# Layer 1's attention in two passes of scores instead of one pass and transposed probabilities

## The chip, the cores and the metric

The program runs on one core of one Trainium2 chip. The metric is device microseconds of one execution, and a kernel's time is the median of several runs. Every operand is fp32.

## The reference, cut to what matters

The input x has 8 batches of 512 tokens of width 128. Two blocks follow each other. Each has an adaptive layer norm, an attention, a second norm and a feed-forward network. The change concerns the attention of the second block (layer 1): 16 heads of width 8, causal, and with a bias that decays with distance.

```python
std_logits = einsum('bhqd,bhkd->bhqk', q, k) * scale
incidence = einsum('bqhp,bkhp->bhqk', read_lines, J_write)      # 6 numbers per head and token
weights = decays[:, None, None] ** diffs_pos[None] * past       # past: key before query
bias = incidence * weights[None] * bias_scale[None, :, None, None]
...
softmax over the causal keys of (std_logits + bias), then times v, then w_out
```

## The kernel before, in words

The stages run one after the other: setup, layer 0's attention, layer 0's quantized feed-forward network, layer 1's attention, layer 1's feed-forward network. X, with all tokens, stays in the on-chip memory from start to end. A scheduler orders the stages except layer 1's attention, whose order is written out by hand in `attention1` (inside `manual_schedule`): on each engine the instructions run in the order in which the Python code issues them.

Layer 1's attention works on 8 batches by 4 groups of four heads. `front1`, once a batch and cut into pieces at its `yield`s, makes the norm, the projections, and from them three packs: for q and k, 32 columns a head, of which 6 hold the lines, 8 the head's numbers (`KR` = 14 in use) and the rest zeros; for v, 9 columns a head, the ninth of them ones, so that the sum of the probabilities falls out of the same matmul.

For a group, `prep1` (L546) turns the packs of q and k, 128x128 at a time, so that the four heads lie at partitions 0, 32, 64 and 96; ACT copies the results to `q1T` and `k1T` (L558, L560); POOL multiplies decays into `qd` (L563) and into four `kd`, one for each tile of 128 queries (L572). `lines1` multiplies the lines of each diagonal tile on PE (`pi`, L584); DVE multiplies by the diagonal's weights (`bias`, L590), and POOL writes -1e30 above the diagonal (L594). `scores1` (L605) computes scores with queries in rows. A head contracts 14 rows only, and heads at different partitions can run side by side in the array.

The 512 queries of a head are four tiles; causality gives tile t the first t+1 blocks of 128 keys. They are grouped in three units: tiles 0 and 1 together, tile 2, tile 3. `quad` takes two PSUM tiles of two banks for four heads. `softmax1` adds the bias of the diagonal tile on DVE (L622, L626), reduces to the negated maximum on DVE (L629), and takes the exponential on ACT, one instruction for each head and tile, with the maximum as the activation's bias (L633). For the product with v the keys must lie in rows: `turn1` transposes the probabilities on PE (`pr1T`, L646), ACT copies them back (`p1T`, L652), and `values1` (L663) contracts them with the pack of v. There, four heads write four strips of 32 partitions of `po`. `outcome1` copies `po` to `og`, turns it (`ogT`, L159), divides by the sums, and after the fourth group multiplies by w_out (L695) and adds to X.

PSUM has eight banks: four for the two pairs of `quad`, two for `tp`, two for `acc`. In the hand-written order, the scores of one unit stand on PE ahead of the transposes of the unit before it, two units being in flight; the parts of `front1` for the next batch and of `outcome1` for the group before lie in between.

Of the kernel before, what the change touches and what calls it, by code (L numbers as in the profile page):

```python
# [32 lines left out]
def kernel(ctx: ExitStack, tc: tile.TileContext, a: dict, out: bass.AP):  # L33
# [3 lines left out]


    ps = ctx.enter_context(tc.tile_pool(name="ps", bufs=2, space=PSUM))
    four = None  # L40
# [4 lines left out]
    def quad(name):  # L45

        return [
            four.tile([P, 2, 512], F32, tag=f"pair{i}", bufs=1, name=f"{name}_{i}")
            for i in range(2)
        ]  # L50

    def tp(name):
        return ps.tile([P, 512], F32, tag="tp", bufs=2, name=name)

    def acc(name):
        return ps.tile([P, 512], F32, tag="acc", bufs=2, name=name)
# [20 lines left out]
    banks = tc.tile_pool(name="ps_l0", bufs=4, space=PSUM)  # L77
# [64 lines left out]
    def ln_norm(pool, tag, stats, b):  # L142
        mv, rstd = stats[b // (B // 2)]
        n = pool.tile(
            [P, NT, D], F32, tag="n", bufs=1 if tag == "a1" else 2, name=f"n_{tag}_{b}"
        )
        for t in range(NT):
            i = (b % (B // 2)) * NT + t
            nc.vector.tensor_scalar(
                n[:, t, :], X[:, b * NT + t, :], mv[:, i, 0:1], rstd[:, i : i + 1],  # L150
                ALU.subtract, ALU.mult,
            )
        return n
# [241 lines left out]
    def lines_setup(pool):  # L395
# [12 lines left out]
        io = pool.tile([P, 384], F32, tag="pT", bufs=8, name="io")  # L408
# [4 lines left out]
        iq = pool.tile([P, P], F32, tag="pT", bufs=8, name="iq")  # L413
# [4 lines left out]
        df = pool.tile([P, P], F32, tag="pT", bufs=8, name="df")  # L418
# [24 lines left out]

        packs = {}
        for i in range(2):
            for name in ("q", "k"):
                pk = pool.tile(
                    [P, NT, H, 32], F32, tag=f"pack_{name}{i}", bufs=1, name=f"pack_{name}{i}"
                )
                nc.gpsimd.memset(pk, 0.0)  # L450
                packs[name, i] = pk
# [6 lines left out]
    UNITS = (((0, 0), (1, P)), ((2, 0),), ((3, 0),))  # L458

    def front1(pool, st, b, stats, bqs, packs):  # L460
# [6 lines left out]
        st["wo", b] = wo = pool.tile([P, D], F32, tag="wo", name=f"wo1_{b}")  # L467
# [14 lines left out]
        for t in range(NT):  # L482
            cur = hT[:, 1 + t * P : 1 + (t + 1) * P]
            pb = acc(f"pb_{b}_{t}")
            nc.tensor.matmul(
                pb[:, 0:64], lhsT=hT[:, t * P : (t + 1) * P], rhs=wC, start=True, stop=True
            )
            nc.tensor.matmul(pb[:, 64:256], lhsT=cur, rhs=wB, start=True, stop=True)
            nc.scalar.copy(pw[:, :, t, :], pb[:, 0:256].rearrange("p (i r) -> p i r", i=2))
            if t % 2:  # L490
                yield
# [13 lines left out]
        nc.gpsimd.tensor_sub(ln, ln, m2)  # L505
        for t in range(NT):
            cur = hT[:, 1 + t * P : 1 + (t + 1) * P]
            pa = acc(f"pa_{b}_{t}")
# [11 lines left out]
            if t == 1:  # L520
                nc.scalar.activation(m2, ln, AF.Square)
                ss = pool.tile([P, nln], F32, tag="ss", bufs=1, name=f"ss_{b}")
                nc.vector.tensor_reduce(ss, m2, AX.X, ALU.add)
                nc.vector.tensor_scalar_max(ss, ss, 1e-24)
            yield

        lg = pool.tile([P, nln], F32, tag="lg", bufs=1, name=f"lg_{b}")
        nc.scalar.activation(lg, ss, AF.Ln)
        rn = pool.tile([P, NT, 2, H], F32, tag="rn", bufs=1, name=f"rn_{b}")
        rv = rn.rearrange("p t w h -> p (t w h)")  # L530
        nc.scalar.activation(rv, lg, AF.Exp, scale=-0.5)
        nc.gpsimd.tensor_mul(lg, rv, rv)
        nc.gpsimd.tensor_mul(lg, lg, ss)
        nc.gpsimd.tensor_scalar(lg, lg, -0.5, 1.5, ALU.mult, ALU.add)
        nc.gpsimd.tensor_mul(rv, rv, lg)
        nc.gpsimd.tensor_mul(
            rn[:, :, 1, :], rn[:, :, 1, :], bsc.unsqueeze(1).to_broadcast([P, NT, H])
        )
        yield
        lnv = ln.rearrange("p (t w h) e -> p t w h e", t=NT, w=2)  # L540
        over = lambda w: rn[:, :, w, :].unsqueeze(3).to_broadcast([P, NT, H, NL])
        nc.gpsimd.tensor_mul(kp[:, :, :, 0:NL], lnv[:, :, 0], over(0))

        nc.gpsimd.tensor_mul(qp[:, :, :, 0:NL], lnv[:, :, 1, :, ::-1], over(1))
        yield

    def prep1(pool, st, b, g, packs, dk, dq):

        qp, kp = packs["q", b % 2], packs["k", b % 2]
        pq, pk = tp(f"pqT_{b}_{g}"), tp(f"pkT_{b}_{g}")  # L550
        for src, dst in ((qp, pq), (kp, pk)):
            for t in range(NT):
                nc.tensor.transpose(
                    dst[:, t * P : (t + 1) * P],
                    src[:, t, 4 * g : 4 * g + 4, :].rearrange("p h e -> p (h e)"), ident,
                )
        qT = pool.tile([P, T], F32, tag="qT", name=f"q1T_{b}_{g}")
        nc.scalar.copy(qT, pq)  # L558
        kT = pool.tile([P, T], F32, tag="kT", name=f"k1T_{b}_{g}")
        nc.scalar.activation(kT, pk, AF.Copy, scale=rowsgn[:, 0:1])  # L560

        qd = pool.tile([P, NT, P], F32, tag="qd", name=f"qd_{b}_{g}")
# [4 lines left out]
        kd = []  # L567
        for t in range(NT):
            kd.append(
                pool.tile([P, (t + 1) * P], F32, tag=f"kd{t}", name=f"kd{t}_{b}_{g}")  # L570
            )
            nc.gpsimd.tensor_mul(kd[t], kT[:, : (t + 1) * P], dk[:, g, 384 - t * P :])  # L572
        st["prep", b, g] = qT, kT, qd, kd

    def lines1(pool, st, b, g, wdiag):


        qT, kT = st["prep", b, g][:2]
        pi = quad(f"pi_{b}_{g}")
        for t in range(NT):  # L580
            tile_t = slice(t * P, (t + 1) * P)
            for j in range(4):
                rl = slice(32 * j, 32 * j + NL)
                nc.tensor.matmul(  # L584
                    pi[j // 2][:, j % 2, tile_t], lhsT=qT[rl, tile_t], rhs=kT[rl, tile_t],
                    start=True, stop=True,
                )
        st["bias", b, g] = bias = pool.tile([P, 4, NT, P], F32, tag="bias", name=f"bias_{b}_{g}")
        for j in range(4):
            nc.vector.tensor_mul(  # L590
                bias[:, j], pi[j // 2][:, j % 2].rearrange("p (t k) -> p t k", k=P),
                wdiag[:, 4 * g + j, :].unsqueeze(1).to_broadcast([P, NT, P]),
# [6 lines left out]
    def scores1(st, b, g, u):  # L599
        qT, kT, qd, kd = st["prep", b, g]  # L600
        st["s", b, g, u] = s = quad(f"s1_{b}_{g}_{u}")
        for t, at in UNITS[u]:
            for j in range(4):
                rk = slice(32 * j, 32 * j + KR)
                nc.tensor.matmul(  # L605
                    s[j // 2][:, j % 2, at : at + (t + 1) * P], lhsT=qd[rk, t, :],
                    rhs=kd[t][rk, :], start=True, stop=True,
                )

    def softmax1(pool, st, b, g, u, i):  # L610

        s, bias, unit, two = st["s", b, g, u][i], st["bias", b, g], UNITS[u], slice(2 * i, 2 * i + 2)
        if i == 0:
            st["pr", b, g, u] = (
                pool.tile([P, 4, T], F32, tag="pr", name=f"pr1_{b}_{g}_{u}"),
                pool.tile([P, 2, 4], F32, tag="nm", bufs=4, name=f"nm1_{b}_{g}_{u}"),
            )
        pr, nm = st["pr", b, g, u]
        if len(unit) == 2:

            diag = s.rearrange("p j (n c) -> p j n c", c=2 * P)[:, :, :, 0:P]
            nc.vector.tensor_add(diag, diag, bias[:, two, 0:2, :])  # L622
        else:
            t = unit[0][0]
            diag = s[:, :, t * P : (t + 1) * P]
            nc.vector.tensor_add(diag, diag, bias[:, two, t, :])  # L626
        for n, (t, at) in enumerate(unit):
            end = at + (t + 1) * P
            nc.vector.tensor_reduce(nm[:, n, two], s[:, :, at:end], AX.X, ALU.max, negate=True)  # L629
        for j in (2 * i, 2 * i + 1):  # L630
            for n, (t, at) in enumerate(unit):
                end = at + (t + 1) * P
                nc.scalar.activation(  # L633
                    pr[:, j, at:end], s[:, j % 2, at:end], AF.Exp, bias=nm[:, n, j : j + 1]
                )

    def width1(u):
        t, at = UNITS[u][-1]
        return at + (t + 1) * P

    def turn1(pool, st, b, g, u, j):

        pr, width = st["pr", b, g, u][0], width1(u)
        pt = tp(f"pr1T_{b}_{g}_{u}_{j}")
        for c in range(0, width, P):
            nc.tensor.transpose(pt[:, c : c + P], pr[:, j, c : c + P], ident)  # L646
        pT = pool.tile([P, T], F32, tag="pT", bufs=8, name=f"p1T_{b}_{g}_{u}_{j}")
        st["pT", b, g, u, j] = pT, pt

    def turned1(st, b, g, u, j):  # L650
        pT, pt = st["pT", b, g, u, j]
        nc.scalar.copy(pT[:, : width1(u)], pt[:, : width1(u)])  # L652
# [247 lines left out]
```

## Time and profile before

| what | value |
|---|---|
| median of 3 runs | 1687.89 us (1687.46 to 1688.57) |
| the profiled execution's own time | 1685.65 us |
| its span | 1683.6 us |
| granted TensorE clock over the span | 0.803 |
| span from 528.6 to 1360.0 us (layer 1's attention) | PE busy 710.27, DVE 427.78, ACT 482.70, POOL 293.20 us, clock 0.76 |
| first and last copy of `po` to `og` (32 of them) | start at 530.0 and 1359.3 us |
| matmul records of `pr1T`, of `s`, of `po` in layer 1's attention | 1280, 1024, 2560 |
| copies of `p1T` on ACT | 384 |

How to read it: the profile lists, for each engine, when an instruction started and how long it took, and what ended the idle time before it. PE is TensorE, PEld its loading of weights. Matmuls are pipelined, and their recorded lengths overlap, so busy time on PE is more than its work; the distance from one start to the next shows the rate. The clock of a stretch is the share of TensorE's full speed that was granted there. The first stages, up to about 460 us, and the last one, from about 1360 us, stand outside the attention of layer 1.

### The profile page before, as it was taken

To read this page: it belongs to the slowest core of one execution; us is meant where nothing else is said; L and a number is where in the kernel's file an instruction comes from. 1 tells how busy PE (TensorE), PEld (TensorE's weight loads), DVE (VectorE), ACT (ScalarE), POOL (GpSimd) and SP (SyncE) were. 2 spreads that over 40 slices of the span, in tenths; PEclk is the share of its full clock that TensorE was granted. 3 is DMA by queue.
4 is the path that set the end of the run, shared out by engine and by line. 5 is a ranking of instruction groups with operands and counts; after the bars stand their busy time and mean duration, and the time that the engine had idled before them with its cause. 6 is when DMAs were issued, how large, how long until landed. Compare 5 with 4: busy or idle time off the path is not lost.

```text
span 1683.6 us, 22090 instructions
## 1 busy us (share of the span) xinstructions
PE 1317.8 (78%) x8644; PEld 814.0 (48%) x8644; DVE 753.9 (45%) x1545; ACT 719.1 (43%) x1440; POOL 428.5 (25%) x524
## 2 busy tenths in 40 slices
PE   4699343553448888988888888888888889999999
PEld 4355132433335555555555555555555544444444
DVE  3866854454425555455555555455545541003000
ACT  3243211221346555655555665555556552114111
POOL 0210322111254424343343244342432200000000
PEclk9799677676757777677687877777777789999999
DMA  6000000000000000000000000000000000000000
GB/s 178 1 1 0 1 0 0 0 0 0 0 0 1 1 1 1 1 1 1 1 1 1 2 1 1 1 1 1 1 1 2 1 1 1 13 7 7 7 7 12
DMA packets 14317, 10.96 MB, mean 7 GB/s; under 512 B 1862, under 2 KB 12678, under 8 KB 14214
## 3 DMA queue, kind: packets, MB, share of 16 engines
q1 hardware_dynamic: 12054, 8.02, 1.6%
q10 hardware_dynamic: 2160, 1.54, 0.3%
q8 instruction: 68, 1.11, 0.3%
q14 instruction: 35, 0.29, 0.1%
HBM read 7.46 MB, written 2.10 MB: 6 GB/s over the span
## 4 chain that ended last, share of the span: by engine, by line
PE 52%; ACT 13%; DVE 4%; POOL 2%; issue 2%; ACTq 0%; POOLq 0%; DVEq 0%
PE ph L814 13%; PE pr1T L646 11%; PE s L605 9%; ACT pr L633 7%; PE po L663 4%; ACT p1T L652 2%; PE pi L584 2%; PE ogT L159 2%; PE pg L794 2%; PE py L825 2%; PE pu L795 2%; DVE nm L629 1%; PE pa L509 1%; ACT k1T L560 1%; PE py L695 1%
## 5 line engine op out<-in xcount | busy, mean ns | idle before, releaser
L652 ACT COPY p1T<-pr1T 128x384 f32<-128x384 f32 (+1 forms) x384 | 195.7, 522 | 247.7 <-PE pr1T L646 247.4
L646 PE MATMUL pr1T<-ident,pr 128*128 128x128 f32 x1280 | 273.0, 369 | 23.7 <-ACT p1T L652 16.9
L605 PE MATMUL s<-kd,qd 14*128 14x128 f32 (+3 forms) x1024 | 196.5, 600 | 80.2 <-ACT pr L633 62.1
L646 PEld LDWEIGHTS pr1T<-ident,pr 128*128 128x128 f32 x1280 | 198.8, 187 | 110.8 <-ACT p1T L652 49.9
L633 ACT ACTIVATE pr<-s,nm 128x128 f32<-128x128 f32 (+3 forms) x512 | 234.6, 547 | 3.0 <-DVE nm L629 2.9
L814 PE MATMUL ph<-g,c_h 128*128 128x512 f32 x512 | 222.0, 592 | 0.0
L629 DVE TENSOR_REDUCE nm<-s 128x2 f32<-128x256 f32 (+3 forms) x256 | 205.0, 821 | 6.6
L814 PEld LDWEIGHTS ph<-g,c_h 128*128 128x128 f32 x512 | 96.4, 190 | 116.7 <-issue 116.7
L605 PEld LDWEIGHTS s<-kd,qd 14*128 14x128 f32 x1024 | 69.7, 224 | 154.4 <-ACT pr L633 69.9
L594 POOL TENSOR_SCALAR_AFFINE_SELECT bias<-bias 128x512 f32<-128x512 f32 x128 | 77.1, 635 | 208.2 <-DVE bias L590 208.2
L818 ACT ACTIVATE g<-ph,c_scl 128x512 f32<-128x512 f32 x64 | 44.0, 688 | 196.3 <-PE ph L814 196.3
L590 DVE TENSOR_TENSOR bias<-pi,wdiag 128x512 f32<-128x512 f32 x128 | 79.4, 683 | 104.3 <-PE pi L584 104.3
L357 PE MATMUL yTp<-ident,q_xn_y 128*88 128x128 f32 x128 | 27.5, 388 | 117.3 <-DVE q_xn_y L252 117.3
L829 DVE TENSOR_TENSOR X<-X,py 128x512 f32<-128x512 f32 x8 | 5.5, 687 | 243.3 <-PE py L825 243.3
L663 PE MATMUL po<-p1T,pack_v 128*32 128x128 f32 x2560 | 108.8, 317 | 0.0
L572 POOL TENSOR_TENSOR kd<-k1T,dk 128x128 f32<-128x128 f32 (+3 forms) x128 | 106.4, 861 | 0.0
L663 PEld LDWEIGHTS po<-p1T,pack_v 128*32 128x32 f32 x2560 | 77.0, 126 | 29.2 <-issue 27.1
L622 DVE TENSOR_TENSOR s<-s,bias 128x512 f32<-128x512 f32 x64 | 44.4, 694 | 85.0 <-PE s L605 85.0
L357 PEld LDWEIGHTS yTp<-ident,q_xn_y 128*88 128x88 f32 x128 | 21.6, 178 | 123.3 <-issue 121.9
L626 DVE TENSOR_TENSOR s<-s,bias 128x256 f32<-128x256 f32 x128 | 54.4, 425 | 58.0 <-PE s L605 53.1
L563 POOL TENSOR_TENSOR qd<-q1T,dq 128x512 f32<-128x512 f32 x32 | 40.4, 1263 | 124.4 <-ACT q1T L558 124.4
L807 POOL TENSOR_TENSOR w3b<-c_w,gs 128x512 f32<-128x512 f32 x8 | 10.1, 1268 | 241.5 <-PE py L825 241.5
(232 smaller groups left out, 1847.8 us busy)
## 6 DMA issues: line engine op xcount, KB each, us to landing
X<-in_x SPq DMA_DIRECT2D x8, 256.0 KB, 6.1
c_h<-in_h SPq DMA_DIRECT2D x2, 1024.0 KB, 10.3
out_x<-X SPq DMA_DIRECT2D x8, 256.0 KB, 2.3
c_wmod<-in_wmod ACTq DMA_DIRECT2D x2, 384.0 KB, 7.0
c_w<-in_w SPq DMA_DIRECT2D x3, 256.0 KB, 3.0
c_wqkv<-in_wqkv ACTq DMA_DIRECT2D x1, 192.0 KB, 7.1
c_bA<-in_bA ACTq DMA_DIRECT2D x1, 192.0 KB, 5.2
c_wA<-in_wA SPq DMA_DIRECT2D x1, 192.0 KB, 4.6
```

Of the source, the lines that this page charges most:

```text
L357: nc.tensor.transpose(pt[:CH0, c * P : (c + 1) * P], q[:, t, c, :], ident)
L572: nc.gpsimd.tensor_mul(kd[t], kT[:, : (t + 1) * P], dk[:, g, 384 - t * P :])
L590: nc.vector.tensor_mul(bias[:, j], pi[j // 2][:, j % 2].rearrange("p (t k) -> p t k", k=P), wdiag[:, 4 * g + j, :].unsqueeze(1).to_broadca ...
L594: nc.gpsimd.affine_select(out=bias[:, j], in_=bias[:, j], compare_op=ALU.is_ge, fill=NEG, base=0, pattern=[[0, NT], [-1, P]], channel_mult ...
L605: nc.tensor.matmul(s[j // 2][:, j % 2, at : at + (t + 1) * P], lhsT=qd[rk, t, :], rhs=kd[t][rk, :], start=True, stop=True,)
L626: nc.vector.tensor_add(diag, diag, bias[:, two, t, :])
L629: nc.vector.tensor_reduce(nm[:, n, two], s[:, :, at:end], AX.X, ALU.max, negate=True)
L633: nc.scalar.activation(pr[:, j, at:end], s[:, j % 2, at:end], AF.Exp, bias=nm[:, n, j : j + 1])
L646: nc.tensor.transpose(pt[:, c : c + P], pr[:, j, c : c + P], ident)
L652: nc.scalar.copy(pT[:, : width1(u)], pt[:, : width1(u)])
L663: nc.tensor.matmul(po[32 * j : 32 * j + 32, t * P : (t + 1) * P], lhsT=vp[:, k, h * VW : h * VW + 32], rhs=st["pT", b, g, u, j][0][:, at + ...
L814: nc.tensor.matmul(ph, lhsT=w[:, k, c * P : (c + 1) * P], rhs=src[:, k, :], start=(k == 0), stop=(k == NC1 - 1),)
```

## The change

The probabilities are no longer transposed. Scores are computed twice. The first pass has queries in rows, as before, and serves for the maxima only: DVE adds the bias and reduces, and the negated maximum of each query and head is written into column 14 (`KR`) of the pack of q (`maxima1`). The pack of k has a column of ones there. The pack of q is then turned once more (`prep_m`), and multiplied by the decays as before (`qm`). The second pass (`scores2`) has keys in rows: 15 rows are contracted, so that the maximum is subtracted within the matmul. Before it, `bank2` writes the diagonal tiles' bias into the same PSUM bank, turned by a PE transpose, and `scores2` accumulates on it. One exponential then covers both heads of a pair and all of a unit (`exp1`), and its result goes straight to `values1`.

The units become tile 3, tiles 2 and 0 together, tile 1. PSUM: two double banks `px` for the first pass and the lines, one double bank `py` for the second pass, one bank `tp`, one bank `po`. `acc` goes: its users in `front1` and `outcome1` take `tp`. Every step is for a pair of heads instead of four.

The order: a round has eight steps; in it the second pass of one group, the first pass of the next and the preparation of the one after run together.

```diff
+    UNITS = (((3, 0),), ((2, 0), (0, 3 * P)), ((1, 0),))
...
+    def bank2(st, b, g, u, i):
+        st["p", b, g, u, i] = p = pair("py", 1, f"s2_{b}_{g}_{u}_{i}")
+        bias = st["bias", b, g, i]
+        for j in range(2):
+            for n, (t, at) in enumerate(UNITS[u]):
+                nc.tensor.matmul(
+                    p[:, j, at + t * P : at + (t + 1) * P], lhsT=bias[:, j, t, :], rhs=ident,
+                    is_transpose=True, start=(n == 0), stop=False, skip_group_check=True,
+                )
+
+    def scores2(st, b, g, u, i):
+        p = st["p", b, g, u, i]
+        for t, at in UNITS[u]:
+            for k in range(t + 1):
+                for j in range(2):
+                    rk = slice(32 * (2 * i + j), 32 * (2 * i + j) + KR + 1)
+                    nc.tensor.matmul(
+                        p[:, j, at + k * P : at + (k + 1) * P],
+                        lhsT=st["kd", b, g][t][rk, k * P : (k + 1) * P],
+                        rhs=st["qm", b, g][rk, t, :], start=False, stop=True,
+                        skip_group_check=True,
+                    )
+
+    def exp1(pool, st, b, g, u, i):
...
+        nc.scalar.activation(pr[:, :, :end], st["p", b, g, u, i][:, :, :end], AF.Exp)
...
+        for n in range(-2, len(groups) + 1):
+            past, second, first, new = (at(n + i) for i in range(-1, 3))
+            if n % NG == NG - 1 and n // NG + 2 < B:
+                front = front1(pool, st, n // NG + 2, stats, bqs, packs)
+            for s in range(8):
+                if s == 0 and second:
+                    prep_m(pool, st, *second, packs, dq)
+                elif s in (1, 5, 6, 7):
+                    next(front, None)
+                elif s == 3 and new:
+                    prep_q(pool, st, *new, packs, dq)
+                elif s == 4 and new:
+                    prep_k(pool, st, *new, packs, dk)
+                if s in (2, 5, 6, 7):
+                    next(ended, None)
+                i = s % 2
+                two = (*second, s // 2 - 1, 1 - i) if second and s > 1 else None
+                if two:
+                    bank2(st, *two)
+                if s < 6 and first:
+                    scores1(st, *first, s // 2, i)
+                elif s > 5 and new:
+                    lines1(st, *new, i)
+                if two:
+                    scores2(st, *two)
+                    exp1(pool, st, *two)
+                if s < 6 and first:
+                    maxima1(st, *first, s // 2, i, packs)
+                elif s > 5 and new:
+                    bias1(pool, st, *new, i, wdiag)
+                if s == 0 and past:
+                    values1(st, *past, 2, packs)
+                    ended = outcome1(pool, st, *past)
+                    next(ended)
+                elif s in (4, 6) and second:
+                    values1(st, *second, s // 2 - 2, packs)
```

Smaller edits go with it. The norm of layer 1's attention moves from DVE to ACT (`ln_norm`, four activations a batch). `front1` computes the lines' reciprocal norms ahead of the projection of q, k and v instead of behind it, so that Square, Ln and Exp stand together on ACT. `kd` has three buffers, `bias` five of a pair each. The activation table with both Ln and Exp is loaded ahead of the attention and held in program order. The PSUM pools `tp` and `acc`, which lasted for the whole program, are now made in each stage, with the same number of banks outside of layer 1's attention.

## Prediction

> **What bounds the kernel now.** I read the page first: engine shares, then the slices with the clock that TensorE was granted, then the groups.
>
> ```profile
> PE 1317.8 (78%) x8644; PEld 814.0 (48%) x8644; DVE 753.9 (45%) x1545; ACT 719.1 (43%) x1440; POOL 428.5 (25%) x524
> ...
> PEclk9799677676757777677687877777777789999999
> ...
> PE 52%; ACT 13%; DVE 4%; POOL 2%; issue 2%; ACTq 0%; POOLq 0%; DVEq 0%
> ...
> L652 ACT COPY p1T<-pr1T 128x384 f32<-128x384 f32 (+1 forms) x384 | 195.7, 522 | 247.7 <-PE pr1T L646 247.4
> L646 PE MATMUL pr1T<-ident,pr 128*128 128x128 f32 x1280 | 273.0, 369 | 23.7 <-ACT p1T L652 16.9
> ```
>
> PE is busiest and leads the chain that ended last; the copies of p1T wait for PE, not the reverse. From slice 12 to 32, layer 1's attention, the clock is about 0.76. The view of stretches puts numbers on it; its columns are the stretch and its length, then busy time and records of PE, PEld, DVE, ACT and POOL, the granted clock, and DMA:
>
> ```profile
> 528.60:1360.00 831.40, 710.27 (x6321) 457.50 (x6314) 427.78 (x808) 482.70 (x1035) 293.20 (x386) 0.76 0.00 1
> ```
>
> PE is busy 85% of these 831 us, ACT 58%, DVE 51%. The 32 copies of `og` start between 530.0 and 1359.3, so a group takes 829.3/31 = 26.75 us. PE's records overlap, so I measure its work by spacing, in the timeline:
>
> ```profile
> 787.04 0.86 PE L663 MATMUL po<-p1T,pack_v 128*32 128x128 f32 x24
> ...
> 790.36 1.09 PE L646 MATMUL pr1T<-ident,pr 128*128 128x128 f32 x8
> 793.35 1.97 PE L646 MATMUL pr1T<-ident,pr 128*128 128x128 f32 x8 [1.90 <-ACT p1T L652]
> 795.25 1.51 PE L663 MATMUL po<-p1T,pack_v 128*32 128x128 f32 x24
> ...
> 804.15 0.91 PE L605 MATMUL s<-kd,qd 14*128 14x384 f32 x4 [2.02 <-ACT pr L633]
> ```
>
> Eight transposes take 1.09 us at clock 1.0 and 1.97 at 0.5 (a row gives start and length); without the last one's latency (0.27, 0.42) they start every 0.109 and 0.213 us after the first. Call that a wave: 128 columns, one pass. An fp32 matmul is two passes (the 32x16 matmuls of L605 are x1024). `po` issues its four 32-column strips together: 24 in six waves. Scores use 14 rows per head; the four records at 804.15 are two heads by two passes of three waves, 6 x 0.109 + 0.27 = 0.92: two heads run in one wave, four where four banks are free.
>
> The clock moves in steps of 3.41 us. Stretches cut at its steps:
>
> ```profile
> 723.60:727.01 3.41, 3.18 (x13) 2.00 (x11) 3.13 (x7) 2.02 (x5) 0.77 (x1) 0.50 0.01 2
> 727.01:730.43 3.42, 2.99 (x19) 1.77 (x19) 1.25 (x4) 2.67 (x6) 0.00 (x0) 1.00 0.00 0
> ...
> 747.49:750.91 3.42, 1.18 (x7) 0.36 (x5) 1.75 (x4) 3.42 (x10) 2.83 (x4) 1.00 0.00 0
> 750.91:754.32 3.41, 3.19 (x11) 1.86 (x11) 0.42 (x2) 0.16 (x1) 3.41 (x4) 0.50 0.00 0
> ```
>
> The first holds transposes and is followed by 1.0; the third holds little but narrow score matmuls and is followed by 0.5. I weighted every matmul of the trace by the share of rows and columns it uses and by the clock, and summed per step. At clock 1.0, all 225 steps with at least 0.38 of the full array kept it, and all 60 that lost it had at most 0.374. At 0.5, the 61 that won it had at least 0.319, and the 133 that did not at most 0.381. So about 0.375 holds the clock and about 0.35 (0.7 of what clock 0.5 can do) wins it. Narrow score matmuls count little: two heads are 2x14/128 = 0.22 of a wave.
>
> **What the change does to PE, per group.** Waves before: 8 (q, k turned) + 34 (scores; unit 0 in fours 6, the others mostly in twos 28) + 8 (lines) + 40 (pr turned) + 20 (values) + 4 (ogT) + 14 (front and end, a quarter batch) = 128. After: 12 (q, k, and q with the maxima) + 40 (scores1 in twos) + 16 (lines in twos) + 16 (bias turned in `bank2`) + 40 (scores2, ten key blocks by two passes by two pairs) + 20 + 4 + 14 = 162. It takes out 40 full waves and puts in 20 full ones and some 54 narrow ones.
>
> Changing between full transposes, row strips and column strips costs extra: from `po` to `pi` the next start comes after 0.203 instead of 0.109, and the second is late too; I take 0.17 at clock 1.0 and 0.25 at 0.5. The Trainium skill (TensorEngine Tiling (Array Packing), Key Properties) says a change of mode drains the engine, without a price. Before has some 11 changes, after 19: `bank2` stands ahead of row strips in each of six steps. By its rule a change could cost a whole latency (0.27, 8 x 0.27 = 2.2 us); by the row 8 x 0.17 = 1.4. I use the row.
>
> PE's own work: before 128 x 0.109 + 1.9 = 15.8 us at 1.0, 30.0 at 0.5. After 162 x 0.109 + 3.2 = 20.9, or 162 x 0.213 + 4.8 = 39.3.
>
> **A new wait.** `py` has one buffer, so each `bank2` waits for the exp of the step before, and scores1 of the next group is queued behind it on PE. The gap is last latency 0.16, the exp, and about 0.1 of semaphores. The exp on 1024 columns is in no row: exps of 384 and 512 have means 0.597 and 0.704, so 1.12 by slope, at most 2 x 0.70; I take 1.12, and 0.70 for 512. Gaps: 4 x 1.38 + 2 x 0.96 = 7.4 us. Cover, in order ahead of the next `bank2`: q and k turned, values of units 0 and 1, the front's pieces, some 4.5 us. So 3 us stay: a group takes about 24 us at clock 1.0. At 0.5 the cover is longer than most gaps: 39.3 + 1.7 = 41.
>
> **What leaves or moves beside PE.** ACT loses 12 copies (4 x 0.586 + 8 x 0.490 = 6.3 us a group) and 16 exps (8.75) for six exps (5.9), gains a copy of mT (0.59) and a quarter of the norm (4 x 0.39 / 4). ACT falls by 8 us a group; being 58% busy and behind PE, it gives nothing by itself. The short waits in which PE had to have `tp` back from a copy go; the exp gap is late in their place. DVE keeps its adds, reduces and bias (13 us). POOL gains qm (1.26): 11.7 us a group. qm is queued behind two affine_selects of 0.635 and is needed by scores2 two steps on, under at least 3 us of scores1 and values; uncovered it would cost 1.3. Maxima written into the pack in strides: nearest row the same reduce, 0.42 to 1.22, so between nothing lost and some 0.05 each on DVE, which has slack; I take nothing. Accumulating onto a turned bias: nearest row `po` for its later keys, no dearer; nothing. Table loads: of 16 loads of 1.28 us at L528 and L531 in the batches, four stay: a gain of 0 to 15 us. Against it, Square and both rsqrt exps now stand on ACT ahead of an exp and wait for POOL's sub (1.8) and DVE's reduce (0.94): a loss of 0 to 4 us a batch. I set both against each other. No DMA moves. Layer 0 and the last FFN keep their order but for one swap; PSUM pools by stage: within 3 us either way.
>
> **The clock after.** Full-wave equivalents per group: before 86 full + 10.3 narrow = 96; after 66 + 19.7 = 86. In steps 2 and 3 (ogT 4, bank2 2+2, q 4, 32 narrow waves worth 7.2) there are 19.2 equivalents, 2.05 us, in 7.7 us: 0.27. That is below 0.375 for more than two clock steps, so the clock falls in every group. It comes back only where values (8), front (0 to 8) and bank2 (4) fall into one clock step of 16 slow waves; 11 are needed. This happens for most groups with a front piece there and few without. Even if it always came back after step 4, step 4 and half of step 3 would run at 0.5: 24 + 4 = 28 us.
>
> Here a rule speaks the other way: the Trainium skill (TensorE: Matmul & The Clock Gate, Part 4) says a PE transpose does not count as PE-busy for the clock. Then swapping transposes for matmuls would not cool it, and the share f of time at 1.0 would stay at 0.53 (clock 0.76). A group takes 1/(f/24 + (1-f)/41): 29.8 us. The stretch at 723.60 contradicts it: twelve transposes, 73% of that slow step, and the clock rose. So I take f = 0.3, clock 0.65: 33.8 us.
>
> Sum: 31 x (33.8 - 26.75) = +219; a deeper pipeline (a group's lines and first scores run one round earlier) adds about 10. The profiled execution: span 1683.6, time 1685.65; plus 229 is 1915. The median of the runs is 2.2 above it; I say 1916.
>
> **Rivals.**
> 1. Clock unchanged (f = 0.53): 29.8 us, +95 + 10: 1791. For: values cluster with the front. Against: the two thin steps. Chance 0.22.
> 2. Clock lost nearly all the time (f = 0.1): 38.3 us, +358 + 10: 2054. For: evenly mixed work at 0.5 uses only 86 x 0.107/41 = 0.22 of the array. Against: the clusters. Chance 0.13.
> 3. Faster: PE, no longer waiting for copies, stays dense and keeps its clock, as in the last slices of the page. It turns at f = 0.75 (26.75 us); at f = 0.9 it is 25 us, -54 + 10: 1644. Against: 0.27 in steps 2 and 3. Chance 0.10.
> That the transposes would stay is excluded: the program holds no pr1T any more.
> The forecast, f about 0.2 to 0.45 (1830 to 1980), has 0.53; no change 0.02.
>
> **Numbers.** 0.2% (about 3.4 us) is what a measurement can tell from no change. Slower 0.88, same 0.02, faster 0.10. The range leaves out rival 3 and half of rival 2: from the 28 us group (1688 + 39 + 10 = 1737) to 2035.
>
> **What would show it.** Right: the attention's clock near 0.65, gaps on PE ahead of `bank2` ended by ACT's exp, each group at 32 to 36 us, ACT far less busy. Wrong: a clock at 0.76 or above there; row strips spaced wider or closer than one wave for two heads; PE waiting for DVE's maxima instead of exp.

## The result and the profile after

The changed kernel takes 1761.07 us (median of 4 runs, 1759.34 to 1765.06) where the kernel before takes 1688.23 us on the same chip: ratio 1.0435, 95% interval 1.0416 to 1.0453. It is slower, as forecast, but by 73 us instead of 228. The times of e3_after_rows32, e4_no_reload, e10_lines32_behind and e12_lines32_front_behind below spread by 2 to 5% from run to run; the ratios leave the longer runs out, and no line or figure of a left-out run's profile is used. The kernel before took 1687.1 to 1688.2 us beside each set of runs, so that times of different sets can be set against each other.

These are the lines of the page after that answer to those shown of before: shares of the engines, the clock by slices, the chain that ended last, and four groups of instructions.

```profile
PE 1451.8 (83%) x10564; PEld 949.4 (54%) x10564; DVE 748.5 (43%) x1521; ACT 508.9 (29%) x773; POOL 470.3 (27%) x558
...
PEclk9899566767555676677876678555556659999999
...
PE 62%; ACT 7%; POOL 3%; DVE 2%; issue 1%; ACTq 0%; POOLq 0%; DVEq 0%
...
L699 ACT ACTIVATE pr<-s 128x1024 f32<-128x1024 f32 (+1 forms) x192 | 169.1, 881 | 498.8 <-PE s L685 498.8
L645 PE MATMUL s<-kd,qd 14*128 14x512 f32 (+3 forms) x1024 | 286.7, 679 | 2.0 <-DVE pack_q L662 0.8
L685 PE MATMUL s<-qm,kd 15*128 15x128 f32 x2560 | 279.0, 373 | 0.0
...
L673 PE MATMUL s<-ident,bias 128*128 128x128 f32 x512 | 131.5, 376 | 54.1 <-ACT pr L699 52.5
```

PE leads the chain by more than before (62% against 52%), and ACT's busy time has fallen by 210 us. PE's only wait of weight in layer 1's attention is that of the bias transposes (L673) for the exponential, 52.5 of their 54.1 us of idle time. The slices of the attention hold many fives: half clock.

The 32 copies of `og` start between 563.0 and 1432.9 us. The stretch between them, with the columns of the view of stretches as before:

```profile
563.00:1433.00 870.00, 810.63 (x8076) 571.67 (x8076) 411.25 (x769) 273.69 (x380) 316.87 (x395) 0.66 0.01 1
```

A group takes 869.9/31 = 28.06 us where it took 26.75, at clock 0.66 where it had 0.76. The span grew by 1759.5 - 1683.6 = 75.9 us, in three parts: 31 periods, +40.6; what lies ahead of the first copy of `og`, 563.0 - 530.0 = +33.0; what lies behind the last, 326.6 - 324.3 = +2.3.

### The profile page after: what moved, and what is told of

It is laid out like the page before. It is cut to its first block, busy times and chain, and to the rows that moved or that the text cites. A ratio compares the mean times of both kernels' runs of the same rounds, so it can differ in the third digit from the quotient of the medians.

```text
span 1759.5 us, 24938 instructions
## 1 busy us (share of the span) xinstructions
PE 1451.8 (83%) x10564; PEld 949.4 (54%) x10564; DVE 748.5 (43%) x1521; ACT 508.9 (29%) x773; POOL 470.3 (27%) x558
## 4 chain that ended last, share of the span: by engine, by line
PE 62%; ACT 7%; POOL 3%; DVE 2%; issue 1%; ACTq 0%; POOLq 0%; DVEq 0%
PE ph L859 12%; PE s L645 11%; PE s L685 8%; PE po L710 6%; PE s L673 6%; ACT pr L699 5%; PE pi L619 4%; PE pa L549 2%; PE pg L839 2%; PE ogT L165 2%; PE py L870 2%; PE pu L840 2%; PE pmT L577 2%; POOL kd L600 1%; PE pb L508 1%
## 5 line engine op out<-in xcount | busy, mean ns | idle before, releaser
L699 ACT ACTIVATE pr<-s 128x1024 f32<-128x1024 f32 (+1 forms) x192 | 169.1, 881 | 498.8 <-PE s L685 498.8
L645 PE MATMUL s<-kd,qd 14*128 14x512 f32 (+3 forms) x1024 | 286.7, 679 | 2.0 <-DVE pack_q L662 0.8
L685 PE MATMUL s<-qm,kd 15*128 15x128 f32 x2560 | 279.0, 373 | 0.0
L685 PEld LDWEIGHTS s<-qm,kd 15*128 15x128 f32 x2560 | 231.3, 263 | 2.5 <-issue 2.5
L659 DVE TENSOR_TENSOR s<-s,bias 128x256 f32<-128x256 f32 (+1 forms) x192 | 100.0, 521 | 266.2 <-PE s L645 156.1
L662 DVE TENSOR_REDUCE pack_q<-s 128x2 f32<-128x1024 f32 (+3 forms) x256 | 205.3, 823 | 6.6
L673 PE MATMUL s<-ident,bias 128*128 128x128 f32 x512 | 131.5, 376 | 54.1 <-ACT pr L699 52.5
L645 PEld LDWEIGHTS s<-kd,qd 14*128 14x128 f32 x1024 | 120.4, 269 | 63.0 <-issue 54.4
L673 PEld LDWEIGHTS s<-ident,bias 128*128 128x128 f32 x512 | 80.0, 188 | 105.3 <-ACT pr L699 87.6
L710 PE MATMUL po<-pr,pack_v 128*32 128x128 f32 x2560 | 130.7, 362 | 0.7 <-ACT pr L699 0.7
L600 POOL TENSOR_TENSOR kd<-k1T,dk 128x512 f32<-128x512 f32 (+3 forms) x128 | 106.4, 866 | 74.6 <-ACT k1T L594 74.6
L619 PE MATMUL pi<-k1T,q1T 6*128 6x128 f32 x1024 | 99.9, 352 | 0.8 <-ACT k1T L594 0.8
```

The lines of the kernel that those rows point to most:

```text
L619: nc.tensor.matmul(pi[:, j, tile_t], lhsT=qT[rl, tile_t], rhs=kT[rl, tile_t], start=True, stop=True,)
L645: nc.tensor.matmul(s[:, j, at : at + (t + 1) * P], lhsT=st["qd", b, g][rk, t, :], rhs=st["kd", b, g][t][rk, :], start=True, stop=True,)
L659: nc.vector.tensor_add(diag, diag, tiles)
L662: nc.vector.tensor_reduce(packs["q", b % 2][:, t, h : h + 2, KR], s[:, :, at : at + (t + 1) * P], AX.X, ALU.max, negate=True,)
L673: nc.tensor.matmul(p[:, j, at + t * P : at + (t + 1) * P], lhsT=bias[:, j, t, :], rhs=ident, is_transpose=True, start=(n == 0), stop=False ...
L685: nc.tensor.matmul(p[:, j, at + k * P : at + (k + 1) * P], lhsT=st["kd", b, g][t][rk, k * P : (k + 1) * P], rhs=st["qm", b, g][rk, t, :], ...
```

## Where the waves went: two passes side by side

The forecast counted 162 waves a group. This is one step of the changed kernel at half clock, in the timeline of PE (start, length, then the instruction): the first pass (L645) of one group and the second (L685) of another.

```profile
1202.70 0.63 PE L673 MATMUL s<-ident,bias 128*128 128x128 f32 x2
1203.27 1.01 PE L645 MATMUL s<-kd,qd 14*128 14x384 f32 x2
1203.30 1.01 PE L685 MATMUL s<-qm,kd 15*128 15x128 f32 x6
1204.07 0.85 PE L645 MATMUL s<-kd,qd 14*128 14x384 f32 x2
1204.10 0.85 PE L685 MATMUL s<-qm,kd 15*128 15x128 f32 x6
1204.71 0.42 PE L645 MATMUL s<-kd,qd 14*128 14x128 f32 x2
1204.74 0.42 PE L685 MATMUL s<-qm,kd 15*128 15x128 f32 x2
1204.92 0.42 PE L645 MATMUL s<-kd,qd 14*128 14x128 f32 x2
1204.95 0.42 PE L685 MATMUL s<-qm,kd 15*128 15x128 f32 x2
```

All matmuls of L645 in a step are issued ahead of all of L685, yet the first of L685 start 0.03 us after the first of L645, and the two go on in turn. They take 1203.27 to 1205.37, 2.1 us, or 8 waves of 0.213 us plus the last one's 0.42. The forecast had 8 waves for each pass, one behind the other. The reason stands in the order: the second pass takes the pair `1 - i`, the first the pair `i`, so that they use different row strips of the array, and nothing lies between them on PE. Four strips run at once. By the same count steps 2 and 3 save 8 waves each, steps 4 and 5 four each, steps 6 and 7 (the lines with the second pass) four each: 32 waves a group. So it is 130, not 162; before has 128.

**e1_same_pair** takes the sharing away and leaves the rest:

```diff
-                two = (*second, s // 2 - 1, 1 - i) if second and s > 1 else None
+                two = (*second, s // 2 - 1, i) if second and s > 1 else None
```

> The second pass takes the same pair of heads as the first pass of its step (i instead of 1 - i); everything else of the changed kernel stays. My theory: the forecast counted the two passes and the lines as separate waves (162 a group), while in the changed kernel they lie in opposite row strips and run four at a time (130). With the same pair they cannot share, so 32 waves a group come back: 32 x (0.109 to 0.213) = 3.5 to 6.8 us a group, 1870 to 1980 us in all, where the blind forecast (1916) stood. Rival, the wait for the exp or the table loads set the pace: 1761 within 1%.

Measured: 2015.36 us (ratio to before 1.1938, 1.1909 to 1.1966), 254 us over the changed kernel. The stretch between its first and last copy of `og`:

```profile
566.78:1686.49 1119.71, 1088.34 (x8076) 780.59 (x8076) 412.40 (x769) 277.12 (x380) 316.86 (x395) 0.56 0.00 1
```

The same 8076 matmul records, 36.1 us a group, and a clock of 0.56. So the 254 us hold two things, the waves and the clock that fell with them; e6 below parts them.

**e9_bank2_behind** keeps the pairs and parts the two passes on PE:

```diff
-                if two:
-                    bank2(st, *two)
                 if s < 6 and first:
                     scores1(st, *first, s // 2, i)
...
                 if two:
+                    bank2(st, *two)
                     scores2(st, *two)
```

> The changed kernel with one move on PE: in each step the bias transposes of the second pass stand behind the first pass's scores (or the lines) instead of ahead of them, so that they come between the two sets of row strips. The pairs stay complementary, nothing is added or left out. Theory (the two passes share waves because they stand next to each other on PE): the sharing ends, 32 waves a group come back, 162 instead of 130, the clock falls below 0.62 in the attention; against this the first pass now covers part of the wait for the exponential, up to 2.5 us a group. 33 to 36 us a group, 1910 to 2010 us. Rival A (only the choice of the pair matters, not the neighbourhood on PE; the wait for the exponential is the larger price): the sharing stays, the cover is won: 26 us a group, 1690 to 1740 us. Rival B: both matter little, within 15 us of the changed kernel.

Measured: 2071.02 us (1.2269, 1.2209 to 1.2328). Its timeline of PE, and its stretch between the copies:

```profile
853.37 2.08 PE L645 MATMUL s<-kd,qd 14*128 14x384 f32 x8
855.38 0.69 PE L673 MATMUL s<-ident,bias 128*128 128x128 f32 x2
855.99 2.08 PE L685 MATMUL s<-qm,kd 15*128 15x128 f32 x16
```

```profile
570.30:1748.10 1177.80, 1171.55 (x8076) 786.20 (x8076) 412.56 (x769) 278.11 (x379) 317.68 (x395) 0.54 0.00 1
```

The same 8 and 16 records as in the rows above now take 2.08 us each, one set behind the other. PE is busy 1171.55 of 1177.80 us: of its waits for the exponential 4.8 us are left, and still a group takes 38.0 us. Neighbourhood on PE decides, not the pair alone; rival A of this run is out. It came out some 60 us above the top of the expected times, at a clock of 0.54.

**e10_lines32_behind** makes the same move in the version e5 below:

> The same move in the fastest version so far (both passes and the lines contract 32 rows, 1596 us, 22.9 us a group, clock 0.89). Theory: 32 waves a group come back, 3.5 us at full clock; two strips at a time use half the rows of a wave, so that the clock falls as well, to 0.7 to 0.8; the cover for the exponential gives up to 2.5 us back: 26 to 30 us a group, 1690 to 1820 us. Rival A (the wait for the exponential is the larger price and the sharing stays): 20.5 us a group, about 1520 us. Rival B (clock stays at 0.89): 24 us a group, about 1630 us.

Measured: 1780.65 us (1702.13 to 1788.54). All its runs lie in the theory's range and well above both rivals, but the spread allows no finer reading.

## The clock: what holds it and what brings it back

The forecast weighted matmuls by the rows and columns they use. If that share decides the clock, contracting all 32 rows of a strip must raise it, at the same number of waves, although the added rows hold zeros.

**e3_after_rows32**: both passes contract 32 rows. A second, masked decay keeps an old maximum in column 14 out of the first pass.

```diff
-                rk = slice(32 * (2 * i + j), 32 * (2 * i + j) + KR)
+                rk = slice(32 * (2 * i + j), 32 * (2 * i + j) + 32)
...
-                    rk = slice(32 * (2 * i + j), 32 * (2 * i + j) + KR + 1)
+                    rk = slice(32 * (2 * i + j), 32 * (2 * i + j) + 32)
...
+        nc.vector.tensor_scalar_mul(dq0, dq, rowsgn[:, 3:4])
```

> The changed kernel with 32 rows contracted in both passes of scores; the column of maxima is kept out of the first pass by a zero in its decays, the other added rows are zeros. Theory that the clock follows the rows in use: activity rises from 86 to about 108 full waves a group, the clock in the attention from 0.66 to 0.8 or more, and a group from 28.1 to 24 or 25 us: 1640 to 1680. Rival, rows do not count: 1761 within 0.5%, clock 0.66.

Measured: 1623.16 us (1604.38 to 1632.48; 0.9585, 0.9523 to 0.9648), 138 us below the changed kernel and faster than before.

```profile
560.01:1298.45 738.44, 662.88 (x8076) 466.48 (x8076) 410.54 (x769) 273.92 (x379) 317.09 (x395) 0.83 0.01 2
```

The same records, clock 0.83 instead of 0.66, 23.8 us a group instead of 28.06.

**e5_lines32** adds to it that the lines contract 32 rows too, with one ACT copy more a group (a `kL` in which all rows but the lines' are zero):

```diff
+        nc.scalar.activation(kL, pt, AF.Copy, scale=rowsgn[:, 4:5])
...
-                rl = slice(32 * (2 * i + j), 32 * (2 * i + j) + NL)
+                rl = slice(32 * (2 * i + j), 32 * (2 * i + j) + 32)
```

> The changed kernel with 32 rows in both passes of scores, and now in the lines too: ACT makes a second copy of the turned k in which only the rows of the lines are not zero, so that the lines can contract all 32 rows of a strip. Clock theory: another 16 x 2 x 26/128 = 6.5 full waves of activity a group (108 to 114), and ACT has room for one copy of 0.7 us; the clock in the attention rises from about 0.85 to about 0.9, the time falls from 1623 to 1590 to 1610. Rival, the wait for the exp and PE's own waves are what is left: 1623 within 0.7%.

Measured: 1595.91 us (0.9456, 0.9442 to 0.947): it beats both kernels, with 22.9 us a group.

```profile
558.75:1267.69 708.94, 630.67 (x8076) 447.46 (x8076) 409.65 (x769) 291.12 (x408) 317.27 (x395) 0.88 0.01 2
```

**e2_before_rows32** does it to the kernel before (its scores contract 32 rows, `KR` replaced by 32 in one slice):

> The kernel before, with its score matmuls contracting 32 rows instead of 14; the added rows are zeros in both packs, the result is the same, and the number of instructions too. Theory that the granted clock follows the share of rows in use: the activity of a group rises from 96 to about 107 full waves, the clock in the attention from 0.76 to about 0.83, and the time falls to 1610 to 1660. Rival, rows do not count (or only those with data that toggle): 1688 within 0.3%, clock 0.76.

Measured: 1671.74 us (0.9913, 0.9889 to 0.9936), clock 0.80 instead of 0.76. The direction was right; the gain of 16 us fell short of the expected 28 to 78. By the forecast's count full matmuls make up 86 of the 96 full waves' worth there (66 of 86 in the changed kernel), so that the scores' rows have less to add; why the clock rose by less than the expectation made of this count is not shown.

**e6_same_pair_rows32** is e3 with the pair of e1:

> The version with 32 rows in both passes, but with the second pass on the same pair of heads as the first pass of its step. It prices the sharing of strips where the clock is held better. My theory: 32 more waves a group at 0.109 to 0.213, with the clock held near 0.8, so 4 to 5 us a group or 125 to 155 us over the 1623: 1750 to 1780. If what the sharing saves was mostly the clock and not the waves, it stays under 1680.

Measured: 1892.78 us (1.1215, 1.1199 to 1.1232), above the expected times.

```profile
563.96:1563.84 999.88, 951.97 (x8076) 681.93 (x8076) 411.36 (x769) 275.75 (x379) 317.17 (x395) 0.66 0.00 1
```

I had reckoned too little for the clock: two strips of 32 rows fill half the array's rows, four fill all of them, and without the sharing it fell from 0.83 to 0.66. That makes a pair with the changed kernel, though the rows contracted differ: both at 0.66, 162 waves take 32.3 us a group and 130 take 28.06. At one clock the 32 waves are thus worth 4.2 us a group, 130 us in 31 periods, about half of what e1 lost; the rest of e1's 254 us went with its clock.

**Where the clock is lost.** I weighted every clock step of 3.41 us of the changed kernel as in the forecast: for each record its share of rows times its share of columns times 0.107 us for each 128 columns that it streams, summed and divided by 3.41. Between the first and the last copy of `og`, the 67 steps that kept full clock use at least 0.368 of the array, and the 14 that lost it at most 0.368; the 160 that stayed at half clock use at most 0.367, and the 14 that ended it at least 0.382. So one share of about 0.37 parts them both ways. In e5, with its rows of zeros counted like others, the 15 steps that lost the clock use at most 0.365 and the 144 that kept it at least 0.372; counted without the zero rows, that border would lie near 0.26.

The forecast put the loss in steps 2 and 3. The view of stretches of the changed kernel, cut at the clock's steps of 3.41 us:

```profile
861.31:864.73 3.42, 2.90 (x36) 2.05 (x34) 3.32 (x7) 0.90 (x1) 2.75 (x4) 1.00 0.00 0
864.73:868.14 3.41, 2.62 (x35) 2.04 (x34) 2.84 (x5) 2.23 (x4) 1.26 (x1) 1.00 0.02 5
871.55:874.97 3.42, 3.38 (x48) 2.91 (x52) 1.13 (x2) 1.15 (x2) 3.34 (x5) 1.00 0.02 5
874.97:878.38 3.41, 1.40 (x46) 1.01 (x38) 1.43 (x3) 1.06 (x2) 1.04 (x1) 1.00 0.00 0
```

The first two are steps 2 and 3 of a round. They use 0.44 and 0.41 of the array, not 0.27: their narrow matmuls stand in half the waves, and the clock holds. It is lost after the fourth, at 0.27: PE is busy for 1.40 us and then waits. ACT and PE there:

```profile
876.04 0.84 ACT L531 ACTIVATE m<-ln 128x768 f32<-128x768 f32 x1 [2.37 <-POOL ln L530]
878.16 0.31 ACT L471 ACTIVATE lg<-ss 128x128 f32<-128x128 f32 x1 [1.28 <-DVE ss L534]
878.50 0.31 ACT L472 ACTIVATE rn<-lg 128x128 f32<-128x128 f32 x1
878.72 0.58 ACT L699 ACTIVATE pr<-s 128x512 f32<-128x512 f32 x1
```

```profile
879.35 0.69 PE L673 MATMUL s<-ident,bias 128*128 128x128 f32 x2 [2.98 <-ACT pr L699]
```

The exponential's scores were ready at about 875.3. It stands on ACT behind the Square of the next batch's lines, which waits 2.37 us for POOL, and behind the Ln, which waits 1.28 for DVE. PE's transposes have lost 2.98 us, and the new rows are at half clock (0.69 for two). Of the 14 clock steps in which the clock was lost, 12 hold such a wait for an exponential, of over 1 us, or its start; the other two hold no wait.

**e11_front_behind** takes that chain out of the way:

```diff
-                elif s in (1, 5, 6, 7):
+                elif s == 1:
                     next(front, None)
...
                     exp1(pool, st, *two)
+                if s > 4:
+                    next(front, None)
```

> The changed kernel with one move: in steps 5, 6 and 7 the next batch's front piece is issued behind the step's exponential instead of ahead of its bias transposes; nothing is added or left out. In the changed kernel, once a batch, Square, Ln and Exp of the lines' norms stand on ACT ahead of step 6's exponential and wait for POOL and DVE: that exponential, whose scores are ready at 875.3 us, starts at 878.72, PE stands for 2.98 us in the one clock step (874.97) with PE busy 1.40 of 3.41, and the next steps run at clock 0.5 until 905. Theory (these waits for the exponential, and not the thin score steps, lose most of the clock): 8 x 2.5 us of waits go and one of the two cold stretches of a batch, some 27 us at half clock that are 16 at full, about 11 us a batch: 1650 to 1700 us, clock of the attention above 0.70. Rival A (the clock is lost a little later in any case, in the next group): only the waits go, 1735 to 1750 us. Rival B (the forecast's steps 2 and 3 lose the clock): within 10 us of the changed kernel.

Measured: 1866.26 us (1.1105, 1.1039 to 1.1171). The theory fell, and both rivals with it.

```profile
562.80:1537.50 974.70, 922.72 (x8076) 644.39 (x8076) 410.94 (x769) 275.55 (x382) 317.92 (x396) 0.57 0.00 1
```

PE's waits at L673 for the exponential went down, from 50.9 us in the changed kernel's attention to 32.7. Other waits came in: 10.2 us of `pmT` for the front's `pack_v` on DVE and `pw` on ACT, 3.2 of the scores for `bias`. And the clock went down too, to 0.57. It is not lost more often (half clock in 14 stretches instead of 15), but a stretch lasts 60 us on average instead of 40. So the rows to look at are those where the changed kernel wins its clock back. Changed kernel:

```profile
901.68 1.94 PE L710 MATMUL po<-pr,pack_v 128*32 128x128 f32 x32
903.55 1.65 PE L549 MATMUL pa<-c_wA,hT 128*128 128x384 f32 x2
904.99 0.94 PE L673 MATMUL s<-ident,bias 128*128 128x128 f32 x4
905.86 0.48 PE L645 MATMUL s<-kd,qd 14*128 14x256 f32 x2
```

e11, at the same place of its order:

```profile
900.58 1.94 PE L710 MATMUL po<-pr,pack_v 128*32 128x128 f32 x32
902.45 1.12 PE L673 MATMUL s<-ident,bias 128*128 128x128 f32 x4
903.49 0.80 PE L645 MATMUL s<-kd,qd 14*128 14x256 f32 x2
```

Values, front and bias transposes stand together in one clock step (902.27 to 905.69, 0.46 of the array by my weights), and the next row is at full clock (0.48 us for its two score matmuls, not 0.80). In e11 the front's `pa` has moved behind the scores; its step from 901.26 uses 0.34, and half clock goes on. So where they stood, the pieces of the front on PE were worth more, as work that brings the clock back, than the waits that they caused. One move changed both and brought new waits, so what the chain on ACT costs by itself was not separated.

**e12_lines32_front_behind** makes the same move in e5, where narrow matmuls already fill the array:

> The same move in the fastest version so far (both passes and the lines contract 32 rows, 1596 us, clock 0.88, PE waits 63 us in all for exponentials there, 2.97 us once a batch behind the lines' norms). Theory: 20 us of waits go, and some 5 us a batch of half clock behind them: 1540 to 1580 us. Rival A (only the waits go): 1575 to 1585 us. Rival B (the move takes cover away elsewhere): 1590 us or more.

Measured: 1579.68 us (0.9282, 0.9255 to 0.931), runs from 1563.76 to 1605.41. The median lies at the upper end of the theory's range and in rival A's too, and the runs reach past both, so the two are not told apart; since e5's 1595.91 lies inside the spread, a gain over e5 is likely but not settled. In the profiled execution (1563.76 us) the clock between the copies of `og` is 0.95, and a group takes 22.1 us. The move that costs 105 us at clock 0.66 costs nothing in e12.

**e4_no_reload**: the changed kernel runs at half clock from about 1151 to 1345 us for several groups on end (0.51 there). I suspected activation table loads.

```diff
-        nc.scalar.activation(sd, mv[:, :, 1], AF.Sqrt, bias=eps[:, 0:1])
+        root = nc.scalar.activation(sd, mv[:, :, 1], AF.Sqrt, bias=eps[:, 0:1])
+        if tag == "f1":
+            tc.keep_in_program_order(root)
```

> The changed kernel with the square root of the last stage's norm held behind the attention on ACT, so that no activation table is loaded inside the attention (six loads of 1.28 us go). Theory that the table loads push the program out of step with the clock's 3.41 us and hold it at 0.51 from 1151 to 1345 us: that stretch goes back to the 27.1 us a group of the earlier one, about 1715 to 1725. Rival, the loads cost only themselves: 1753 to 1759.

Measured: 1765.05 us (1739.61 to 1804.56; 1.0318, 1.0296 to 1.034). Inconclusive: its runs lie on both sides of the changed kernel's 1761, from 21 us below to 43 above, and fit neither the theory nor the rival. The changed kernel's own trace says what keeps it at half clock: from 1199.2 to 1346.0 us no clock step uses more than 0.37 of the array, since the values never fall into one step with enough other full matmuls. The step from 1346.0 does hold all 32 records of values with four transposes of `o1T` and three of the bias; it uses 0.45, and full clock follows. What moved the work against the clock's steps is open. The half clock starts at 1090.0, in a wait of 4.29 us for an exponential with two table loads of 1.28 us ahead of it on ACT (2.97 us in the batch before, without loads), but e4 does not show that the loads are the cause.

## What the second pass's own parts cost

Both are edits of e3, and leave work out as their expectations say.

**e7_half_exp**:

```diff
-        nc.scalar.activation(pr[:, :, :end], st["p", b, g, u, i][:, :, :end], AF.Exp)
+        nc.scalar.activation(pr[:, 0, :end], st["p", b, g, u, i][:, 0, :end], AF.Exp)
...
-                        rhs=st["pr", b, g, u, j // 2][:, j % 2, at + k * P : at + (k + 1) * P],
+                        rhs=st["pr", b, g, u, j // 2][:, 0, at + k * P : at + (k + 1) * P],
```

> The version with 32 rows, with the exp of one head of each pair left out (its values use the other head's probabilities), so that the exp that stands before each turn of the bias takes about 0.6 us instead of 1.02. If the wait for the exp on PE's path is real: 4 x 0.4 + 2 x 0.2 = 2 us less gap a group, of which some is under cover: 1570 to 1600. If it is covered: 1623 within 0.7%.

Measured: 1545.61 us (0.9159, 0.9145 to 0.9172), 21.3 us a group, clock 0.89 instead of e3's 0.83. The wait for the exponential is on the path: 2.5 us a group go, more than expected. PE's waits for it fall from 62.6 us in e3 to 39.3, by 0.8 us a group; the clock's rise is worth another 1.3 by the formula of the next part (an estimate), and some 0.4 stay unexplained.

**e8_no_bank2**: the second pass starts its own PSUM banks (`start=True`), and `bank2`'s transposes go.

> The version with 32 rows without the transposes that put the bias into the bank of the second pass (the bias and the causal mask are left out there). It prices these 16 transposes and the changes between full array and row strips that they bring. By the counts: 16 x 0.12 + 12 changes x 0.17 = 4 us a group at an unchanged clock, 1500 to 1530; since they are full waves of activity (108 to 92), the clock may fall, and then 1540 to 1600.

Measured: 1513.63 us (0.896, 0.8933 to 0.8986), 20.1 us a group: 3.7 less than e3, near the count of 4, but not for the transposes alone. The clock rose to 0.87, and the first pass now stands ahead of the wait for the exponential, which falls from 62.6 to 30.7 us, by 1.0 us a group. So the transposes and their changes of mode come to less than was counted; how much less was not separated.

## Why the prediction was right or wrong

**The step that failed** is the sum of PE's waves: "40 (scores1 in twos) + 16 (lines in twos) + 16 (bias turned in `bank2`) + 40 (scores2 ...)", taken as 162 separate waves. The two passes and the lines share 32 of them; I had counted two strips at a time within each line, and not asked which strips the next line on PE uses. The rows from 1203.27 show eight waves for both passes where sixteen were counted. The Trainium skill (TensorEngine Tiling (Array Packing), Key Properties) says that different tiles can load weights and multiply in parallel; from that section I had drawn only that a change of mode drains the engine. The rows from 1203.27 agree with it, across two instructions of different lines.

With 130 waves the forecast's own 24 and 41 us a group become 24 - 32 x 0.109 = 20.5 at clock 1.0 and 41 - 32 x 0.213 = 34.2 at 0.5. With each kernel's measured clock c (f = 2c - 1), T = 1/(f/20.5 + (1-f)/34.2), or with 24 and 41 where the sharing is gone:

| kernel | waves | clock | group by formula, us | measured, us |
|---|---|---|---|---|
| changed | 130 | 0.66 | 28.2 | 28.06 |
| e3 | 130 | 0.83 | 23.7 | 23.8 |
| e5 | 130 | 0.88 | 22.7 | 22.9 |
| e12 | 130 | 0.95 | 21.4 | 22.1 |
| e11 | 130 | 0.57 | 31.3 | 31.4 |
| e6 | 162 | 0.66 | 33.4 | 32.3 |
| e1 | 162 | 0.56 | 37.8 | 36.1 |
| e9 | 162 | 0.54 | 38.8 | 38.0 |

So the price of a wave and the clock's part in it were right within 5%, and the count was wrong: 31 x (33.8 - 28.06) = 178 us too many, of which some 12 are the step from 0.65 to 0.66.

**The second mis-sized term** is the deeper pipeline, "about 10": 33.0 us measured ahead of the first `og`. From the first q turned to the first `og` it is 61.1 us (501.9 to 563.0) where it was 36.9 (493.15 to 530.0), at a clock of 0.52 between 460 and 563 us; the other 8.8 lie ahead of it, in the first front. With +2.3 at the end the parts without a period are 25 us above the forecast. Together: 229 - 178 + 25 = 76, the measured growth of the span.

**The clock** was forecast as 0.65 and measured as 0.66, and that is luck. The forecast took it with 162 waves, and with 162 waves (e1) it is 0.56 and the time 2015 us. There the thin steps do lose it, as forecast: from 1405.16 to 1408.58 us PE of e1 is busy all the time with lines, narrow scores and few transposes, uses 0.27 of the array, and half clock follows. With 130 waves steps 2 and 3 hold it, since the sharing makes them dense; it is lost mostly at waits for the exponential, behind the front's chain on ACT or in groups with no front piece. That it comes back where values, front and bias transposes fall into one clock step was right (e11). That use of rows and columns decides it was right in direction (e3, e5), also for rows of zeros. By the formula the clock is what makes the change a loss: at f = 0.53 (clock 0.76) 130 waves give an estimated 25.3 us a group, 1.4 below before, some 45 us over 31 periods against 35 at the two ends; e3 at 0.83 does beat before.

**Waits.** The gap at `bank2` measures 50.9/31 = 1.6 us a group, forecast 3 at full clock and 1.7 at half; the exponential of 1024 columns takes 1.02, estimated 1.12, that of 512 columns 0.58 to 0.60, taken as 0.70. The short waits for copies did go. "A loss of 0 to 4 us a batch" for Square and the two rsqrt activations was right as a wait (2.98, and 4.29 where two table loads stand in it) and set against the table loads too lightly, for it also falls where the clock is lost.

**Beside PE.** ACT fell from 482.70 to 273.69 us in about the same stretch, 6.7 us a group (forecast 8), and gave nothing by itself. POOL is at 316.87/31 = 10.2 us a group (forecast 11.7; the forecast's own row gives 293.20/31 + 1.26 = 10.7), DVE at 13.3 (13). No wait of PE for POOL's `qm` or for DVE's maxima shows between the first and last copy of `og`, so that these were rightly taken at nothing. The stages outside kept their times: in the first 460 us PE is busy 256.33 us (254.67 before). The price of mode changes was not measured by itself. Of the rivals, the unchanged clock had the nearest time (1791, which like 2054 leaves out the 2.2 us that 1916 counts), but not for its reason: the clock did fall.

## What to carry to other kernels

Count waves over neighbouring instructions on PE, not line by line: ask which row strips the next matmul uses, and put work of the other strips beside it (here 32 waves a group; without them e1 and e9 took 254 and 310 us more, about half of it in e1 through the clock). When a change trades dense matmuls for narrow ones, work out what share of the array each clock step uses, and fill it: contracting the strip's unused rows with zeros took the changed kernel from 1761 to 1596 us. A piece of full matmuls that seems to be in the way may be what brings the clock back (e11), so move it only with the clock in view.

## What the runs showed of the hardware

- In the changed kernel, matmuls of one line start ahead of earlier issued ones of another in other row strips: L685 at 1203.30 ahead of L645 at 1204.92. With two transposes over all rows between them they do not (e9: 853.37 and 855.99).
- Rows of zeros count for the clock as others do: 0.66 to 0.83 (e3), with the border at the same share, about 0.37 (e5).
- In the changed kernel the clock was lost with PE busy 1.40 of 3.41 us, in e11 (853.5 us, 0.36 of the array) with only 0.27 us idle, and in e1 (1405.16 us, 0.27) with none: idleness is not needed.
